# Row transfers by the sync engine at row numbers in registers, and the second tile of the last pair but one rounded as a whole ahead of the last pair's sums

## The chip, the cores and the metric

The kernel runs on one core of a Trainium2 chip. Such a core has a matrix engine (TensorE, PE in the profile, its weight loads PEld), a vector engine (VectorE, DVE), an activation engine (ScalarE, ACT), a general engine (GpSimd, POOL), a sync engine that here only issues transfers (SyncE, SP), and 16 DMA engines that move data between the device's memory and the on-chip memory. Each engine takes its instructions in order; between engines they wait for each other by semaphores. The metric is the device time of one execution in microseconds (us), given as the median of several runs.

## The reference

One gated cross-attention layer of the Flamingo kind, followed by a feed-forward layer with quantised weights and activations. There are 16 batches of 224 rows of 512 values (x), and for every batch 750 context rows of 384 values with a mask. Cut to what matters:

```python
x = x + tanh(g_xattn) * attention(layernorm(x), ctx, mask)      # 8 heads of 64, softmax over the unmasked context rows
x = x + tanh(g_ffn)   * ffn(layernorm(x))

def ffn(x):
    h = gelu(bitlinear(x, w1, b1))          # 512 -> 2048
    return bitlinear(h, w2, b2)             # 2048 -> 512

def bitlinear(x, w, b):
    xq = act_quant(rmsnorm(x))              # per row: scale 127 / max|x|, round, scale back
    wq = weight_quant(w)                    # one scale for the matrix: round to -1, 0, 1
    return xq @ wq.T + b
```

The rounding of a row needs the largest absolute value of the whole row; the mean square of the row only enters a factor that is applied behind the matrix product.

## The kernel before

**Order of the rows.** The program first sorts the 16 batches by how many context rows the mask keeps, and then works on slots (positions in that order) instead of batches. The 3584 rows of the slots, one after the other, are cut into 28 tiles of 128 rows (`NTOK`), and two tiles make a pair (`NPAIR` is 14). A slot has 224 rows, so a tile can hold the end of one slot and the beginning of the next: tiles 1, 3 and 5 of every seven do. `sh.token` is a table on the chip that holds, for each row of each tile, the number of its row in x and in the output. Rows are fetched (`fetch_x`, L807) and stored (`store`, L1488) by indirect transfers of POOL, which take the 128 row numbers of a tile out of that table. Only the last four tiles are stored otherwise: three row numbers are loaded into registers of SP (L1750 to L1759), and L1486 stores the tile from SP in one or two pieces.

**Attention.** A loop over the slots (L1711) weaves three streams of work together (`merge`, by estimated costs): the attention of slot s, the preparation of slots s+1 to s+3 (fetch and normalise x, gather the kept context rows, queries, keys and values), and the feed-forward work of an earlier pair. `scores` (L1095) makes the scores on PE, a masked copy with the row's maximum on DVE, the exponential with the row's sum on ACT, a reciprocal on DVE (L1139), and the scaling of the probabilities `p` by that reciprocal on POOL (L1140). `turn_probs` (L1155) turns `p` on PE (L1163) for the product with the values.

**Feed-forward, per pair.** `residual` fetches the rows of x again into `y` (three buffers, so a fetch must wait until the pair three before is stored) and adds a bias on POOL (L1245). `project` (L1247) multiplies by `wo` on PE (L1252) and adds onto `y` on DVE (L1255). `normalise` (L1277) makes the layer norm and the rounded `xq` on DVE and turns it by a transposing transfer of SP into `xqT` (L1302). `up` (L1324) multiplies on PE (L1333) and adds the bias on DVE (L1341). `gelu` (L1358) applies Gelu on ACT, then on DVE takes the largest absolute value (L1369), scales, rounds into 16-bit integers (L1372) and casts (L1374), giving `hq`, which a transposing transfer of SP turns into `hqT` (L1377); ACT squares the row for the mean square (L1382). `down` (L1465) multiplies on PE (L1469); the result and `y` are added on DVE (L1482), and the tile is stored.

**The tail.** Behind the loop stands the work on the last pairs, written out (L1767 to L1812). Pair 13 has functions of its own: `turn_rows` turns `xq` on PE, `up_last` works by halves of 1024 columns with the maxima by halves (L1419), `gelu_last` makes the rounding from the two maxima, and `turn_by_tensor` (L1347) turns `hq` by 16 PE transposes and two ACT copies (L1355). `mean_square` and `measure_last` make the factor of a tile on ACT and POOL. In pair 12, tile 0 is turned by SP's transfer and tile 1 by `turn_by_tensor`. Below, (12,1) is tile 1 of pair 12.

**Order.** The framework puts each engine's instructions into an order of its own, near the program's; `tc.issue_after(instruction)` makes what is inside come later in that order than the instruction, without a wait on the chip. Waits follow from the data: who reads a tile waits for who wrote it, and who overwrites it waits for its readers. Two stores of rows that are only known at run time count as writes of the same output, so that each waits until the one before has landed.

Of the kernel before, what the change touches and what calls it, by code (L numbers as in the profile page):

```python
# [11 lines left out]
ALU = mybir.AluOpType  # L12
# [722 lines left out]
def compact_path(ctx, tc, sh, x, context, out, late_loads, stages):  # L735
# [71 lines left out]
    def fetch_x(dst, t):  # L807
        nc.gpsimd.indirect_dma_start(  # L808
            out=dst,
            out_offset=None,  # L810
            in_=x_rows,
            in_offset=bass.IndirectOffsetOnAxis(ap=token(t), axis=0),
            bounds_check=B * S - 1,
            oob_is_err=False,
        )
# [177 lines left out]
    def fetch(i):  # L993
        if i:
            xp = pa.tile([P, 2, D], F32, tag="x", name=f"x_{i}", bufs=3)
        else:
            xp = early[:, : 2 * D].rearrange("p (k d) -> p k d", k=2)
        for k in range(2):
            fetch_x(xp[:, k, :], 2 * i + k)
        normed[i] = xp  # L1000
# [237 lines left out]
    def residual(i):  # L1238
# [3 lines left out]
        for k in range(2):  # L1242
            fetch_x(y[:, k, :], 2 * i + k)
# [103 lines left out]
    def turn_by_tensor(i, k):  # L1347
        f = pairs[i]
        hq, hqT = f["hq", k], f["hqT", k]
        for g in range(2):  # L1350
            pt = gen([P, NF // 2, P], BF16, f"hqp_{i}_{k}_{g}")
            for n in range(NF // 2):
                at = g * FF // 2 + n * P
                nc.tensor.transpose(pt[:, n, :], hq[:, at : at + P], ident16)
# [3 lines left out]
    def gelu(i, ks=(0, 1)):  # L1358
# [8 lines left out]
        for k in ks:  # L1367
# [8 lines left out]
            if (i, k) != (NPAIR - 2, 1):  # L1376
                nc.sync.dma_start_transpose(out=hqT, in_=hq)  # L1377
# [14 lines left out]
    def up_last(i, k):  # L1392
# [8 lines left out]
        for g in range(2):  # L1401
# [16 lines left out]
            with tc.issue_after(late["rounded"]):  # L1418
                nc.vector.tensor_reduce(most[:, g : g + 1], h[:, cols], AX.X, ALU.max, apply_absolute_value=True)  # L1419
        f["h", k], f["most", k] = h, most  # L1420
        return last.ins

# [55 lines left out]
    def store(i, k):  # L1478
# [5 lines left out]
        if i >= NPAIR - 2:  # L1484
            for p, n, at in late["pieces"][2 * i + k]:
                nc.sync.dma_start(out_rows[bass.ds(at, n), :], y[p : p + n, :])  # L1486
            return added.ins
        nc.gpsimd.indirect_dma_start(  # L1488
            out=out_rows,
            out_offset=bass.IndirectOffsetOnAxis(ap=token(2 * i + k), axis=0),  # L1490
            in_=y,
            in_offset=None,
            bounds_check=B * S - 1,
            oob_is_err=False,
        )
# [253 lines left out]

    with tc.issue_after(pairs[NPAIR - 6]["turning"].ins):  # L1750
        where = [
            nc.values_load(
                sh.token[p : p + 1, t // 7, t % 7 : t % 7 + 1],
                engines=[mybir.EngineType.SP],
                min_val=0,
                max_val=B * S - n,
            )
            for p, t, n in ((0, NTOK - 4, 64), (64, NTOK - 4, S), (32, NTOK - 2, S))
        ]  # L1759

    late["pieces"] = {
        NTOK - 4: [(0, 64, where[0]), (64, 64, where[1])],
        NTOK - 3: [(0, 128, where[1] + 64)],
        NTOK - 2: [(0, 32, where[1] + 192), (32, 96, where[2])],
        NTOK - 1: [(0, 128, where[2] + 96)],
    }
# [14 lines left out]
    with tc.issue_after(lowered):  # L1781
        for k in range(2):
            projected = project(i, k)
            normed = normalise(i, (k,))
    with tc.issue_after(normed):
        gelu(i - 1, (1,))
    measure_last(i - 1, 1)
    with tc.issue_after(projected):
        lowered = down(i - 1, 0, lambda: turn_rows(i, 0))
    with tc.issue_after(lowered):  # L1790
        up_last(i, 0)
        mean_square(i, 0)
        turn_rows(i, 1)
        raised = up_last(i, 1)
    store(i - 1, 0)
    with tc.issue_after(raised):
        turn_by_tensor(i - 1, 1)
        lowered = down(i - 1, 1)
    mean_square(i, 1)
    with tc.issue_after(gelu_last(i, 0)):  # L1800
        added = store(i - 1, 1)
    with tc.issue_after(added):
        gelu_last(i, 1)
    with tc.issue_after(raised):
        turn_by_tensor(i, 0)
    measure_last(i, 0)
    measure_last(i, 1)
    with tc.issue_after(lowered):
        down(i, 0, lambda: turn_by_tensor(i, 1))
    store(i, 0)  # L1810
    down(i, 1)
# [35 lines left out]
```

## Time and profile before

| | us |
|---|---|
| median of 3 runs | 729.25 (728.92 to 732.07) |
| profiled execution | 730.5, its span 728.4 |
| PE busy | 677.1 of the span |
| DVE, ACT, POOL busy | 495.1, 413.0, 389.3 |
| mean granted PE clock | 0.982 |
| stores by POOL (24) | 27.6 busy, 1.148 each |
| fetches of y and x by POOL (28 and 26) | 29.0 and 28.5 busy, 1.04 and 1.10 each |
| scaling of `p` by POOL (64) | 78.7 busy |

The profile is of one execution. "Busy" counts an engine's own work; a line of a group or of the timeline gives the start, the length, the engine, the line of the kernel, the operation, `output<-input` with shapes, a count, and in brackets how long the engine had stood idle before it and whose end released it. A line of the waits reads: who waited, `<-` for whom, us in total, number of times, the longest. A line of the stretches gives the busy time of each engine in that window, the clock that PE was granted (1.00 is full), the share of time that the DMA engines were busy, and GB/s. Idle time of an engine costs only where something that sets the end waits for it.

### The profile page before, as it was taken

The numbers are of one execution on the slowest core, as the hardware profiler recorded it, in microseconds if no ns is written. First come the engines' busy times: TensorE is split into PE (matmuls) and PEld (weight loads), VectorE is DVE, ScalarE is ACT, GpSimd is POOL, SyncE is SP. The second block draws the span as 40 slices with busy tenths as digits, with TensorE's granted clock in tenths as the row PEclk, the third lists the DMA queues.
The fourth block names the chain that finished last, engine by engine and source line by source line (L and its number), as shares of the span: only waits on it lengthen the run. The fifth ranks groups of instructions, "written<-read, shape, count | busy, mean of one in ns | idle before, by whom it ended". The sixth has DMA issues, their size and how long they took to land.

```text
span 728.4 us, 11444 instructions
## 1 busy us (share of the span) xinstructions
PE 677.1 (93%) x3917; PEld 432.7 (59%) x3917; DVE 495.1 (68%) x1296; ACT 413.0 (57%) x974; POOL 389.3 (53%) x545
## 2 busy tenths in 40 slices
PE   4997899999999999999799999999999999998875
PEld 3775687665666566656465566566666656554332
DVE  5495755877476475775485966747768493969883
ACT  2558554376483672774565647727466564766462
POOL 5583568454484534735646655457555445266512
PEclk9999899999999999999999999999999999999998
DMA  6884031113232222223222332113214232142301
GB/s 231 294 281 157 1 103 35 28 46 58 74 75 58 66 46 62 81 44 88 65 48 76 81 73 69 42 45 94 61 45 69 63 58 73 30 102 56 75 14 49
DMA packets 80146, 56.74 MB, mean 78 GB/s; under 512 B 68208, under 2 KB 68352, under 8 KB 79952
## 3 DMA queue, kind: packets, MB, share of 16 engines
q1 hardware_dynamic: 72336, 31.22, 18.2%
q0 software_dynamic: 7744, 24.71, 10.9%
q8 instruction: 33, 0.54, 0.3%
q14 instruction: 33, 0.27, 0.1%
HBM read 32.06 MB, written 7.34 MB: 54 GB/s over the span
## 4 chain that ended last, share of the span: by engine, by line
PE 70%; DVE 10%; issue 6%; POOL 6%; DMA 3%; ACT 3%; POOLq 0%; DVEq 0%; ACTq 0%
PE op L1252 11%; PE qp L1066 11%; PE fp L1469 11%; PE hp L1333 9%; PE kp L946 6%; PE sim L1106 5%; PE vp L962 5%; PE ptp L1163 3%; PE av L1188 3%; POOL p L1140 2%; DMA hqT<-hq 2%; POOL x L808 2%; PE xnp L1045 1%; DVE a L1369 1%; PE ctxp L935 1%
## 5 line engine op out<-in xcount | busy, mean ns | idle before, releaser
L1140 POOL TENSOR_TENSOR p<-p,rec 112x768 f32<-112x768 f32 (+2 forms) x64 | 78.7, 1230 | 76.2 <-DVE rec L1139 30.7
L1130 ACT ACTIVATE p<-p,nm 112x192 f32<-112x192 f32 (+2 forms) x256 | 104.7, 412 | 9.9 <-DVE nm L1120 6.9
L1469 PE MATMUL fp<-w2T,hqT 128*128 128x512 fp8e4 x448 | 103.3, 384 | 6.2 <-ACT hqT L1355 3.1
L1066 PE MATMUL qp<-xnT,wq_sb 128*128 128x224 f32 x512 | 105.3, 359 | 0.6 <-ACT xnT L781 0.6
L1252 PE MATMUL op<-wo_sb,xoT 128*128 128x512 f32 x224 | 103.7, 599 | 0.0
L1333 PE MATMUL hp<-w1T,xqT 128*128 128x512 fp8e4 x416 | 99.1, 382 | 2.2 <-DVE h L1341 1.0
L1066 PEld LDWEIGHTS qp<-xnT,wq_sb 128*128 128x128 f32 x512 | 97.1, 194 | 6.4 <-issue 3.1
L1341 DVE SCALAR_TENSOR_TENSOR h<-hp,c,b_bc 128x1024 f32<-128x1024 f32 x52 | 66.5, 1281 | 43.6 <-PE hp L1333 43.3
L1469 PEld LDWEIGHTS <-hqT 128*128 128x128 bf16 x448 | 42.9, 99 | 61.2 <-issue 7.0
L1120 DVE CUSTOM_DVE_ANT_0 p<-sim,mask 112x192 f32<-112x192 f32 (+2 forms) x224 | 56.1, 304 | 33.0 <-PE sim L1106 32.5
L1369 DVE TENSOR_REDUCE a<-h 128x1 f32<-128x2048 f32 x26 | 59.3, 2281 | 19.8 <-ACT h L1366 19.6
L1333 PEld LDWEIGHTS <-xqT 128*128 128x128 bf16 x416 | 39.8, 98 | 46.1 <-issue 7.0
L1482 DVE SCALAR_TENSOR_TENSOR y<-fp,c,y 128x512 f32<-128x512 f32 x28 | 20.9, 746 | 64.8 <-PE fp L1469 63.2
L1252 PEld LDWEIGHTS op<-wo_sb,xoT 128*128 128x128 f32 x224 | 40.7, 190 | 38.8 <-issue 36.4
L946 PE MATMUL kp<-ctxT,wk_sb 128*128 128x192 f32 (+1 forms) x360 | 60.4, 317 | 0.0
L1488 POOL DMA_INDIRECT out_dram<-y,token x24 | 27.6, 1148 | 57.9 <-DVE y L1482 53.6
L946 PEld LDWEIGHTS kp<-ctxT,wk_sb 128*128 128x128 f32 x360 | 54.7, 199 | 5.5 <-issue 3.8
L1382 ACT ACTIVATE h<-h 128x2048 f32<-128x2048 f32 x25 | 47.7, 1908 | 17.4 <-DVE hq L1372 12.2
L1312 POOL TENSOR_TENSOR y<-y,b_bc 128x512 f32<-128x512 f32 x28 | 36.9, 1321 | 34.5 <-DVE fx L1292 34.2
L781 ACT COPY pT<-ptp 128x448 f32<-128x448 f32 (+1 forms) x62 | 32.2, 535 | 40.3 <-PE ptp L1163 38.8
L781 ACT COPY qT<-qp 128x448 f32<-128x448 f32 x29 | 15.4, 532 | 66.4 <-PE qp L1066 66.1
L1106 PE MATMUL sim<-kT,qT 64*112 64x192 f32 (+2 forms) x512 | 50.9, 312 | 2.3 <-issue 0.9
(199 smaller groups left out, 1249.5 us busy)
## 6 DMA issues: line engine op xcount, KB each, us to landing
raw<-in_L_ffn_w_dram SPq DMA_DIRECT2D x16, 512.0 KB
wq_sb<-in_L_xattn_W_q_dram SPq DMA_DIRECT2D x1, 1024.0 KB
b_bc<-in_L_ffn_b_dram SPq DMA_DIRECT2D x1, 1024.0 KB
wk_sb<-in_L_xattn_W_k_dram SPq DMA_DIRECT2D x1, 768.0 KB
wv_sb<-in_L_xattn_W_v_dram SPq DMA_DIRECT2D x1, 768.0 KB
wo_sb<-in_L_xattn_W_o_dram SPq DMA_DIRECT2D x1, 512.0 KB
wo_sb<-in_L_xattn_W_o_dram SPq DMA_DIRECT2D x2, 256.0 KB
out_dram<-y SPq DMA_DIRECT2D x2, 256.0 KB
```

The source lines that it names most:

```text
L946: nc.tensor.matmul(pk[:, p - p0, :], lhsT=sh.wk[:, c, p * P : (p + 1) * P], rhs=st["ctxT"][:, c, :cap], start=(c == 0), stop=(c == NC - 1),)
L1066: nc.tensor.matmul(pq[:, i, :], lhsT=sh.wq[:, d, (p + i) * P : (p + i + 1) * P], rhs=st["xnT"][:, d, :], start=(d == 0), stop=(d == ND - 1),)
L1106: nc.tensor.matmul(sim[:, j, i, :cap], lhsT=st["qT"][j * DH : (j + 1) * DH, p, q * TQ : (q + 1) * TQ], rhs=keys["kT"][j * DH : (j + 1) * D ...
L1120: nc.vector.tensor_tensor_reduce(out=probs[:, h, :cap], in0=sim[:, j, i, :cap], in1=keys["mask"][:, first + j * begin : first + j * begin ...
L1130: nc.scalar.activation(probs[:, h, :cap], probs[:, h, :cap], AF.Exp, bias=nmax, scale=-1.0, accum_out=total[:TQ, h : h + 1],)
L1140: nc.gpsimd.tensor_tensor(probs[:, :, first : first + cap], probs[:, :, :cap], rec[:TQ].unsqueeze(2).to_broadcast([TQ, 4, cap]), ALU.mult,)
L1252: last = nc.tensor.matmul(po, lhsT=xoT[:, d, at : at + P], rhs=sh.wo[:, d, :], start=(d == 0), stop=(d == ND - 1))
L1333: last = nc.tensor.matmul(ph[:, n, :], lhsT=f["xqT"][:, k * ND + d, :], rhs=w1T[:, d, at : at + NB], start=(d == 0), stop=(d == ND - 1),)
L1341: nc.vector.scalar_tensor_tensor(h[:, cols], ph.rearrange("t i n -> t (i n)"), f["c1", k], sh.b1[:, cols], ALU.mult, ALU.add)
L1369: nc.vector.tensor_reduce(amax[:, k : k + 1], h, AX.X, ALU.max, apply_absolute_value=True)
L1382: nc.scalar.activation(f["h", k], f["h", k], AF.Square, accum_out=ss[:, k : k + 1])
L1469: last = nc.tensor.matmul(po, lhsT=f["hqT", k][:, n, :], rhs=w2T[:, n, :], start=(n == 0), stop=(n == NF - 1))
```

## The change

Three things change.

1. A new generator `pieces_of(t)` gives, for a tile, its one or two pieces that lie in one slot each. The first time that a slot is touched, the number of its first row is loaded from `sh.token` into a register of SP (`begins`). `fetch_x` gets a flag: with it, the rows come by direct transfers of SP at these numbers. It is set for x from tile 7 on and for every fetch of `y`. All stores go this way too. The three register loads behind the loop and the table of pieces go.
2. In the tail, `gelu(12,1)` comes before the sums and the normalising of pair 13 and not behind them. Its `hq` is now turned by SP's transfer, and that of (12,0) by PE, between the two projections of pair 13.
3. The maxima of pair 13 become a function `maxima` of their own, placed behind both `up_last`; the squares of pair 13 are placed later; `turn_rows(13,0)` and the turning of (13,1) no longer stand in the middle of another tile's `down`, but between whole ones.

```diff
--- before.py
+++ after.py
@@ -804,7 +804,31 @@
     x_rows = x.rearrange("b s d -> (b s) d")
     out_rows = out.rearrange("b s d -> (b s) d")
 
-    def fetch_x(dst, t):
+
+    begins = {}
+
+    def pieces_of(t):
+
+        p = 0
+        while p < P:
+            s, at = divmod(t * P + p, S)
+            n = min(P - p, S - at)
+            if s not in begins:
+                r = s * S
+                begins[s] = nc.values_load(
+                    sh.token[r % P : r % P + 1, r // P // 7, r // P % 7 : r // P % 7 + 1],
+                    engines=[mybir.EngineType.SP],
+                    min_val=0,
+                    max_val=B * S - S,
+                )
+            yield p, n, begins[s] + at
+            p += n
+
+    def fetch_x(dst, t, sync=False):
+        if sync:
+            for p, n, at in pieces_of(t):
+                nc.sync.dma_start(dst[p : p + n, :], x_rows[bass.ds(at, n), :])
+            return
         nc.gpsimd.indirect_dma_start(
             out=dst,
             out_offset=None,
@@ -996,7 +1020,7 @@
         else:
             xp = early[:, : 2 * D].rearrange("p (k d) -> p k d", k=2)
         for k in range(2):
-            fetch_x(xp[:, k, :], 2 * i + k)
+            fetch_x(xp[:, k, :], 2 * i + k, 2 * i + k >= 7)
         normed[i] = xp
 
     def norm(i, ks=(0, 1)):
@@ -1240,7 +1264,7 @@
         f = pairs[i] = {}
         f["y"] = y = late["rows"].tile([P, 2, D], F32, tag="y", name=f"y_{i}", bufs=3)
         for k in range(2):
-            fetch_x(y[:, k, :], 2 * i + k)
+            fetch_x(y[:, k, :], 2 * i + k, True)
         for k in range(2):
             nc.gpsimd.tensor_tensor(y[:, k, :], y[:, k, :], sh.bo, ALU.add)
 
@@ -1351,7 +1375,7 @@
             pt = gen([P, NF // 2, P], BF16, f"hqp_{i}_{k}_{g}")
             for n in range(NF // 2):
                 at = g * FF // 2 + n * P
-                nc.tensor.transpose(pt[:, n, :], hq[:, at : at + P], ident16)
+                f["turned"] = nc.tensor.transpose(pt[:, n, :], hq[:, at : at + P], ident16).ins
             turned = nc.scalar.copy(hqT[:, g * NF // 2 : (g + 1) * NF // 2, :], pt)
         return turned.ins
 
@@ -1373,7 +1397,7 @@
             f["hqT", k] = hqT = late["rows"].tile([P, NF, P], BF16, tag="hqT", name=f"hqT_{i}_{k}", bufs=2)
             late["rounded"] = nc.vector.tensor_copy(hq, hq.bitcast(I16)).ins
             f["hq", k] = hq
-            if (i, k) != (NPAIR - 2, 1):
+            if (i, k) != (NPAIR - 2, 0):
                 nc.sync.dma_start_transpose(out=hqT, in_=hq)
         if (i, ks[0]) == (NPAIR - 2, 1):
             f["a2", 1] = amax[:, 1:2]
@@ -1415,10 +1439,16 @@
                 h[:, cols], ph.rearrange("t i n -> t (i n)"), f["c1", k], sh.b1[:, cols], ALU.mult, ALU.add
             )
             nc.scalar.activation(h[:, cols], h[:, cols], AF.Gelu)
-            with tc.issue_after(late["rounded"]):
-                nc.vector.tensor_reduce(most[:, g : g + 1], h[:, cols], AX.X, ALU.max, apply_absolute_value=True)
         f["h", k], f["most", k] = h, most
         return last.ins
+
+    def maxima(i, k):
+        f = pairs[i]
+        for g in range(2):
+            cols = slice(2 * g * NB, 2 * (g + 1) * NB)
+            nc.vector.tensor_reduce(
+                f["most", k][:, g : g + 1], f["h", k][:, cols], AX.X, ALU.max, apply_absolute_value=True
+            )
 
     def gelu_last(i, k):
 
@@ -1481,18 +1511,9 @@
         y = f["y"][:, k, :]
         added = nc.vector.scalar_tensor_tensor(y, po, f["c2", k], y, ALU.mult, ALU.add)
         load["v"] += 700
-        if i >= NPAIR - 2:
-            for p, n, at in late["pieces"][2 * i + k]:
-                nc.sync.dma_start(out_rows[bass.ds(at, n), :], y[p : p + n, :])
-            return added.ins
-        nc.gpsimd.indirect_dma_start(
-            out=out_rows,
-            out_offset=bass.IndirectOffsetOnAxis(ap=token(2 * i + k), axis=0),
-            in_=y,
-            in_offset=None,
-            bounds_check=B * S - 1,
-            oob_is_err=False,
-        )
+        for p, n, at in pieces_of(2 * i + k):
+            nc.sync.dma_start(out_rows[bass.ds(at, n), :], y[p : p + n, :])
+        return added.ins
 
     NPAIR = NTOK // 2
 
@@ -1746,24 +1767,6 @@
             scores(s + 1, 0)
             scores(s + 1, 1)
 
-
-    with tc.issue_after(pairs[NPAIR - 6]["turning"].ins):
-        where = [
-            nc.values_load(
-                sh.token[p : p + 1, t // 7, t % 7 : t % 7 + 1],
-                engines=[mybir.EngineType.SP],
-                min_val=0,
-                max_val=B * S - n,
-            )
-            for p, t, n in ((0, NTOK - 4, 64), (64, NTOK - 4, S), (32, NTOK - 2, S))
-        ]
-
-    late["pieces"] = {
-        NTOK - 4: [(0, 64, where[0]), (64, 64, where[1])],
-        NTOK - 3: [(0, 128, where[1] + 64)],
-        NTOK - 2: [(0, 32, where[1] + 192), (32, 96, where[2])],
-        NTOK - 1: [(0, 128, where[2] + 96)],
-    }
     i = NPAIR - 1
     residual(i)
     with tc.issue_after(late["av"]), tc.issue_after(late["rounded"]):
@@ -1778,37 +1781,46 @@
     with tc.issue_after(raised):
         lowered = down(i - 2, 1)
     store(i - 2, 1)
-    with tc.issue_after(lowered):
-        for k in range(2):
-            projected = project(i, k)
-            normed = normalise(i, (k,))
+    gelu(i - 1, (1,))
+    with tc.issue_after(late["rounded"]):
+        with tc.issue_after(lowered):
+            projected = project(i, 0)
+        normed = normalise(i, (0,))
+        with tc.issue_after(projected):
+            turn_by_tensor(i - 1, 0)
     with tc.issue_after(normed):
-        gelu(i - 1, (1,))
+        with tc.issue_after(pairs[i - 1]["turned"]):
+            projected = project(i, 1)
+        normalise(i, (1,))
     measure_last(i - 1, 1)
     with tc.issue_after(projected):
-        lowered = down(i - 1, 0, lambda: turn_rows(i, 0))
+        lowered = down(i - 1, 0)
     with tc.issue_after(lowered):
-        up_last(i, 0)
-        mean_square(i, 0)
+        turn_rows(i, 0)
+        raised = up_last(i, 0)
+    with tc.issue_after(raised):
         turn_rows(i, 1)
         raised = up_last(i, 1)
+    maxima(i, 0)
     store(i - 1, 0)
     with tc.issue_after(raised):
-        turn_by_tensor(i - 1, 1)
         lowered = down(i - 1, 1)
-    mean_square(i, 1)
+    mean_square(i, 0)
     with tc.issue_after(gelu_last(i, 0)):
+        maxima(i, 1)
         added = store(i - 1, 1)
     with tc.issue_after(added):
         gelu_last(i, 1)
-    with tc.issue_after(raised):
+    with tc.issue_after(lowered):
         turn_by_tensor(i, 0)
+        lowered = down(i, 0)
+    mean_square(i, 1)
     measure_last(i, 0)
     measure_last(i, 1)
     with tc.issue_after(lowered):
-        down(i, 0, lambda: turn_by_tensor(i, 1))
+        turn_by_tensor(i, 1)
+        down(i, 1)
     store(i, 0)
-    down(i, 1)
     store(i, 1)
 
 
```

## The prediction

> **What bounds the kernel now.** I read first the busy times, then PE's idle time by releaser, then the stretches around its long gaps, then the tail on PE and SP.
>
> ```profile
> PE 677.1 (93%) x3917; PEld 432.7 (59%) x3917; DVE 495.1 (68%) x1296; ACT 413.0 (57%) x974; POOL 389.3 (53%) x545
> ...
> PE ptp L1163 <- POOL p L1140: 15.8, 11, 4.2
> ```
>
> PE holds 677 of 728.4 us, so a gain must come out of PE's 51 idle us or its slow clock. The largest releaser of idle PE is POOL's scaling of the probabilities (L1140): 15.8 us in 11 waits. By the timeline of PE these are 4.23 us before 60.98, 1.11 before 205.37, 1.40 before 254.96, 1.46 before 302.89, 3.55 and 0.47 before 349.77 and 353.77, 0.97 before 398.13, 0.35, 0.43 and 1.02 between 434 and 453, and 0.78 before 662.58.
>
> The stretches around two of the gaps (length, PE, PEld, DVE, ACT, POOL busy, granted clock, DMA):
>
> ```profile
> 57.00:61.00 4.00, 0.01 (x1) 0.02 (x1) 3.43 (x5) 3.98 (x8) 3.67 (x4) 1.00 0.98 337
> 61.00:66.00 5.00, 5.00 (x34) 3.43 (x35) 1.00 (x3) 2.89 (x5) 1.35 (x1) 0.66 0.37 147
> ...
> 346.00:350.00 4.00, 0.45 (x4) 0.26 (x4) 0.00 (x0) 3.29 (x3) 3.82 (x4) 1.00 0.17 49
> 350.00:355.00 5.00, 4.53 (x20) 2.16 (x18) 1.67 (x2) 1.01 (x3) 4.45 (x6) 0.66 0.39 108
> ```
>
> A gap costs more than itself: the granted clock is 0.66 in the 5 us behind it. What POOL did ahead of the 3.55 us gap:
>
> ```profile
> 337.85 1.09 POOL L1488 DMA_INDIRECT out_dram<-y,token  x1 [4.41 <-DVE y L1482]
> 340.96 1.08 POOL L808 DMA_INDIRECT y<-in_x_dram,token  x1 [2.02 <-DMA out_dram<-y,token]
> 342.35 1.01 POOL L808 DMA_INDIRECT y<-in_x_dram,token  x1 [0.31 <-issue]
> 344.57 1.29 POOL L1245 TENSOR_TENSOR y<-y,bo_bc 128x512 f32<-128x512 f32 x1 [1.21 <-DMA y<-in_x_dram,token]
> ...
> 348.25 1.47 POOL L1140 TENSOR_TENSOR p<-p,rec 112x768 f32<-112x768 f32 x1
> 349.88 1.04 POOL L808 DMA_INDIRECT x<-in_x_dram,token  x1 [0.16 <-issue]
> 351.22 0.99 POOL L808 DMA_INDIRECT x<-in_x_dram,token  x1 [0.30 <-issue]
> 352.24 1.48 POOL L1140 TENSOR_TENSOR p<-p,rec 112x768 f32<-112x768 f32 x1
> ```
>
> The reciprocals that the two L1140 need ended at 343.65 and 345.86 on DVE. POOL came 4.6 and 6.4 us late: it issued row transfers, stood for a store to land, and stood for rows to arrive.
>
> The tail, on PE, DVE and SP:
>
> ```profile
> 689.76 1.90 PE L1469 MATMUL fp<-w2T,hqT 128*128 128x512 fp8e4 x8 [2.26 <-DMA hqT<-hq]
> 702.55 1.07 PE L1354 MATMUL hqp<-ident,hq 128*128 128x128 bf16 x16 [0.83 <-DVE hq L1374]
> 706.02 5.31 PE L1469 MATMUL fp<-w2T,hqT 128*128 128x512 fp8e4 x16 [2.39 <-ACT hqT L1355]
> 717.73 0.75 DVE L1482 SCALAR_TENSOR_TENSOR y<-fp,c,y 128x512 f32<-128x512 f32 x1 [2.85 <-PE fp L1469]
> ...
> 718.51 0.35 SPq L1486 DMA_DIRECT2D out_dram<-y  x1
> 720.63 0.32 SPq L1486 DMA_DIRECT2D out_dram<-y  x1
> 724.62 0.35 SPq L1486 DMA_DIRECT2D out_dram<-y  x1
> ```
>
> PE waits for a transfer that turns hq(12,0), then for hq(12,1), rounded late, then for ACT; the 16 matmuls at 706.02 take 5.31 us where others take 3.63. The end hangs on SP: tile 26 leaves in two pieces 2.12 us apart, and tile 27 only when the second has landed, 3.99 later, although its sum ended at 721.93. So the end is the sum of tile 26 (718.48) plus 9.9 us. Pairs are numbered 0 to 13; (12,0) is the first tile of pair 12.
>
> **The change, part by part.**
>
> Rows off POOL. All 28 y fetches, 24 stores and the 21 x fetches from tile 7 on leave POOL, at 1.04, 1.12 and 1.01 us each, 77 us of POOL. Most lies where nobody waits; what counts is what stands ahead of a late L1140.
> - Gap at 57: two x fetches (tiles 8, 9) hold POOL from 53.95 to 58.18, while the reciprocals were there at 54.22 and 56.81. Without them the second context fetch (0.95) ends about 54.9 and the first L1140 (1.46) about 56.4, ahead of PE's 56.75. Worth 4.23, plus 1.2 for matmuls at the low clock (8 of L1188 took 1.76 where the others take 0.98, 4 of L1163 took 1.01 instead of 0.60). DVE is 9.4 tenths busy there with weights, so I take 4.5 of 5.4.
> - Gaps at 205, 255, 303: the second L1140 stands behind two x fetches (2.4 us with their pauses), its reciprocal 4.7 us old. The gaps are 1.11, 1.40 and 1.46, and ten of L946 behind the first take 3.41 where 1.75 is usual, with more at low clock after them: 2.3. Against it, in these three slots the store that frees y is cut in two (tiles 1, 3, 5 cross a batch), so y comes later (below). I take 2.0, 0.9 and 0.9 of 3.4, 1.4 and 1.46.
> - Gap at 347: the store that frees y (tile 7) is whole. Issued at 337.6, landed 2.1 later (the spacing of the two pieces above), y rows in two pieces landed 2.6 after that, L1245 twice and the context fetch (3.6) end near 346.0, L1140 near 347.4 instead of 349.7; the second near 348.9, before PE's 353.3. 3.55 and 0.47 go down to about 1.2, and with them 1.4 of low clock (8 of L1333 took 2.89 instead of 1.89, L1163 0.96). I take 4.2.
> - 0.97 at 398 and 0.35 at 434: the same kind, 1.3. The two at 450 and 453 follow their reciprocals (448.60, 450.89) at once: nothing. The 0.78 at 662 stands behind POOL arithmetic: nothing.
> Sum: 4.5 + 2.0 + 0.9 + 0.9 + 4.2 + 1.3 = 13.8; the ends are 6 (the x fetches ahead of the gaps from 205 on save nothing, the rest half) and 20 (every gap above with its low clock).
>
> Rows onto SP. Some 110 direct transfers, 6 of them there already, at 0.36 plus two small register steps (0.08), and 16 loads of a row number at 0.44 plus 0.17, about 60 us of SP over the span. SP is idle most of the time: the longest of its waits for an hq cast is 28.7 us. Three waits are new on SP. A cut store's second piece waits for the first to land (2.1 to 2.4); a y fetch waits for its old store (2.0, now POOL's 22.3 us of "POOL y L808 <- DMA out_dram<-y,token"); a fetch of x waits for nothing now. Behind them on SP stand the transposing transfers, and behind those PE. The order in time is kind: at 382.15 the xqT transfer goes out, at 386.2 the second store would, at 388.4 the y fetch, and the next hqT is at 403.5. The closest is a first store at 377.2, just behind the hqT issue at 376.54 and five ahead of xqT, whose matmuls start 7 us later. Two transfers have no slack: PE waits 0.56 at 381.74 and 0.40 at 645.32. Bounds: 0 to 12 us (one us in each of 12 slots); I take 2, nearest to these two waits.
>
> The Trainium skill, "DMA: Bandwidth & Descriptors", section "Issuing engines are not separate DMA queues", speaks against this half: another issuing engine saves only the issue time, which it calls usually small beside the transfer. By it only the 1.0 us issues leave the path, the waits for landings stay, and the gap at 347 would give the shorter issues alone, 2.0 instead of 4.2, the sum 11.6 instead of 13.8. The trace has POOL standing 22.3 us for landings in front of unrelated work, and that wait moves to an engine with nothing urgent behind it, so I keep the trace's sum.
>
> The tail. gelu(12,1) with reduce 2.28, scale 0.37, round 1.29 and cast 0.69 goes ahead of normalise(13,0). DVE is then: cast of (12,0) ends 682.8 as now, that of (12,1) at 687.3 (702.5 now), xq of (13,0) about 691.3 (688.8 now), xq of (13,1) about 695.3 (694.7 now).
> - hq(12,0) is turned by PE (16 transposes, 0.9) between the two projections, and copied by ACT behind the squares at 686 to 688. Its down starts at 688.4 instead of 689.76, runs unbroken to 691.9, and the 2.26 wait goes.
> - up(13,0): turn and copy (0.4 + 0.6) from 692.0, matmuls 693.0 to 696.6; up(13,1): 697.6 to 701.2.
> - hq(12,1) goes by SP's transfer at 687.4; at 6.74 us, as the one at 682.98 took, it lands by 694.2, so down(12,1) runs 701.2 to 704.8. Now it ends at 711.33.
> - DVE then sets the pace: four bias adds at 1.28, two maxima at 1.2, the sum of (12,0) at 0.75, all from 695.3 without a hole, then scale and rounding (2.65): hq(13,0) by 706. Turn, ACT copies (1.0 each), down(13,0) 707 to 711; its factor comes over ACT's squares and six POOL steps, some 5 us from the last square in the trace, at about 712. So the sum of tile 26 ends near 712.4, not 718.48.
> - Turning hq(13,1) is no longer hidden inside down(13,0): 0.5 + 1.0 + 3.6 + 0.75 behind hq(13,1) (711.7) gives 717.5. SP's chain asks for tile 27 only at 712.4 + 2.1 + 4.0 = 718.5, so this is covered by 1 us; without the cover it would cost its excess.
> - The moved maxima and squares are the same instructions, counted above; the removed early loads of row numbers (three of 0.44) lay on an idle SP.
> Gain 6.1. Bounds: -2 (DVE order worse, clock low for 3 us) to 9 (every PE gap after 687 and the slow 1.7).
>
> **Sum.** The profiled execution is 730.5 us (span 728.4 and 2.1 around it), 1.25 above the median of 729.25. 13.8 - 2 + 6.1 = 17.9: 712.6 on its own time, 711.3 on the median's. I say 712.
>
> **The rivals.**
> 1. Only the tail pays. L1140 comes earlier, but PE then stands for ACT's exponentials or DVE, or y arrives later through cut stores and L1245 still stands ahead of L1140. For it: the waits at 450 and 453 followed the reciprocal directly. Against it: elsewhere the reciprocals are 2.8 to 6.4 us old. 730 - 6 - 2 = 722.
> 2. Slower: SP's in-order waits hold the transposing transfers. If the order on SP puts a store or a y fetch ahead of an hqT, that hqT waits 2.1 to 4.5 us, PE with it, in up to 12 slots and twice in a slot. It decides from where the mean delay past the slack exceeds 17.9 + 2 over 12, 1.7 us per slot; at 2.2 us per slot, 730 + 26 - 20 = 736. Against it are the distances named above. [...]
> 3. No change: the two halves give back what they gain (y late at every slot, 14; tail bound by DVE, 6): 729.
>
> **How the numbers follow.** Both halves pay 0.67 (702 to 720); only the tail 0.16 (720 to 725.6); no change 0.06; slower 0.11. A difference under 0.5% (3.6 us) can't be told from none. Faster 0.83, same 0.06, slower 0.11. The low end is 730.5 - 20 - 9 = 702; the high end takes in rival 1 and the slow side of no change, to 728, and leaves out rival 2 and some 0.05 below.
>
> **What would show it.** Right: PE's wait for L1140 falls from 15.8 us to under 5; no POOL transfer for y or output is left; the stretch 57 to 61 is busy at full clock; down(12,1) follows up(13,1) without a gap; the last three stores keep their spacing but begin some 18 us earlier. Wrong: PE idle ended by hqT or xqT in most slots; SP waits for out_dram in front of transposes; L1245 waiting longer for y; a PE gap before the turn of hq(13,0) of over 3 us.

## The result, and the profile after

The changed kernel takes 786.54 us (median; 782.59 to 790.69) against 728.47 us (727.04 to 732.07) for the kernel before: a ratio of 1.0786, with a 95% interval of 1.0759 to 1.0813. It is 58 us slower; the forecast was 712, with a range of 702 to 728. The profiled execution has a span of 784.6 us against 728.4, and a mean granted clock of 0.953 against 0.982. In the changed kernel L1140 has become L1164, L1163 is L1187 (PE's turn of the scaled probabilities), L1245 is L1269, L1255 is L1279, L1312 is L1336, L808 is L830 and L1486 is L1515.

The busy times of the page, and from the waits of all engines (total us, number of waits, longest) four rows that grew and lead to the cause:

```profile
PE 690.8 (88%) x3917; PEld 441.7 (56%) x3917; DVE 490.7 (63%) x1296; ACT 414.5 (53%) x974; POOL 310.5 (40%) x472
...
POOL p L1164 <- DVE rec L1163: 138.3, 26, 17.7
...
PE ptp L1187 <- POOL p L1164: 57.4, 12, 13.1
...
DVE y L1279 <- POOL y L1269: 32.0, 4, 9.0
POOL y L1269 <- DMA y<-in_x_dram: 21.8, 9, 5.9
```

POOL did lose its 79 us of row transfers, 389.3 down to 310.5, and yet PE's wait for POOL's scaling rose from 15.8 to 57.4 us. The 56.2 us of longer span are 42.5 of idle PE (51.3 before, 93.8 now) and 13.7 of longer busy PE, for the same 3917 matmuls at a lower clock; the wait for the scaling alone, up by 41.6, is nearly all of the idle part. The first row of the waits tells that POOL is not the culprit this time: it stands for a reciprocal of DVE (138.3 us, 30.7 before). The last two rows lead on: DVE stands for POOL's y, and POOL for the y rows to arrive.

PE's timeline has the large waits, four of them with a smaller one behind three (start, length, what runs, idle time before it and its releaser):

```profile
160.10 1.01 PE L1187 MATMUL ptp<-ident,p 112*128 112x112 f32 x4 [10.33 <-POOL p L1164]
163.55 1.01 PE L1187 MATMUL ptp<-ident,p 112*128 112x112 f32 x4 [2.06 <-POOL p L1164]
...
227.86 1.01 PE L1187 MATMUL ptp<-ident,p 112*128 112x112 f32 x4 [11.12 <-POOL p L1164]
231.57 1.01 PE L1187 MATMUL ptp<-ident,p 112*128 112x112 f32 x4 [2.32 <-POOL p L1164]
...
294.80 1.01 PE L1187 MATMUL ptp<-ident,p 112*128 112x112 f32 x4 [12.95 <-POOL p L1164]
298.10 1.01 PE L1187 MATMUL ptp<-ident,p 112*128 112x112 f32 x4 [1.92 <-POOL p L1164]
...
552.00 1.01 PE L1187 MATMUL ptp<-ident,p 112*128 112x112 f32 x4 [13.12 <-POOL p L1164]
```

These seven are 53.8 of the 57.4 us. All other waits for the scaling together are 3.6 us, where before they were 15.8: what the prediction wanted to remove was removed, and something larger came in at four places. Two stretches of the prediction, and those around the first large gap (length, PE, PEld, DVE, ACT, POOL busy, granted clock, DMA share, GB/s):

```profile
57.00:61.00 4.00, 3.03 (x28) 2.23 (x26) 4.00 (x5) 4.00 (x13) 2.32 (x2) 1.00 0.93 321
61.00:66.00 5.00, 4.09 (x28) 2.51 (x27) 5.00 (x17) 5.00 (x11) 1.47 (x1) 1.00 0.78 251
...
150.00:160.00 10.00, 0.00 (x0) 0.00 (x0) 5.54 (x11) 4.38 (x18) 5.17 (x4) 0.75 0.27 84
160.00:165.00 5.00, 2.84 (x13) 2.49 (x14) 4.53 (x10) 1.19 (x3) 4.28 (x7) 0.50 0.00 0
165.00:170.00 5.00, 5.00 (x17) 4.18 (x17) 0.00 (x0) 1.53 (x5) 2.91 (x6) 0.64 0.23 52
```

57 to 61, empty on PE before, now has PE busy for 3.03 of 4 us, at full clock. From 150 to 160 PE does nothing at all.

Now the second large gap, followed back through POOL and SP. First SP's waits in the whole run, then its row transfers ahead of the gap with the turn on PE that it waits for, then POOL and DVE:

```profile
SPq L830 <- PE xnp L1069: 115.9, 10, 59.7
...
SPq L1515 <- DMA out_dram<-y: 29.5, 18, 2.9
```

```profile
207.72 2.51 SPq L1515 DMA_DIRECT2D out_dram<-y  x2
...
211.13 0.66 PE L1069 MATMUL xnp<-ident,x 128*128 128x128 f32 x4 [0.57 <-ACT ctxT L781]
...
211.91 1.42 SPq L830 DMA_DIRECT2D x<-in_x_dram  x3
213.53 1.74 SPq L830 DMA_DIRECT2D y<-in_x_dram  x3
...
218.72 2.49 POOL L1269 TENSOR_TENSOR y<-y,bo_bc 128x512 f32<-128x512 f32 x2 [3.90 <-DMA y<-in_x_dram]
...
220.02 0.75 DVE L1279 SCALAR_TENSOR_TENSOR y<-op,tgates,y 128x512 f32<-128x512 f32 x1 [8.42 <-POOL y L1269]
...
224.94 0.17 DVE L1163 RECIPROCAL rec<-sum 112x4 f32<-112x4 f32 x1
...
226.33 1.48 POOL L1164 TENSOR_TENSOR p<-p,rec 112x768 f32<-112x768 f32 x1
```

Read from the end: PE resumes at 227.86 when POOL has scaled p. POOL could not before DVE's reciprocal at 224.94 and a bias add of its own that stood ahead (1.27 us). DVE had stood 8.42 us at the sum of projection and y (L1279), which stands ahead of the reciprocal in its order. The sum waited for POOL's y + b_o, that for the y rows, and these were asked for at 213.53, directly behind the x fetch. The x fetch waits for an x buffer: there are three, and the last reader of the one it will overwrite is PE's turn xnp, which ends at 211.79 here, 0.12 us before the fetch. So SP stands ten times for PE, 115.9 us in all and 59.7 at the longest (in front of 146.62), and what is behind x on SP stands with it: y. Before the change POOL asked for pair 0's y at 102.34; now SP asks for it at 148.37.

### The profile page after: what moved, and what is told of

Same layout as the page of the kernel before. It is cut to its first block, busy times and chain, and to the rows that moved or that the text cites. A ratio compares the mean times of both kernels' runs of the same rounds, so it can differ in the third digit from the quotient of the medians.

```text
span 784.6 us, 11697 instructions
## 1 busy us (share of the span) xinstructions
PE 690.8 (88%) x3917; PEld 441.7 (56%) x3917; DVE 490.7 (63%) x1296; ACT 414.5 (53%) x974; POOL 310.5 (40%) x472
## 4 chain that ended last, share of the span: by engine, by line
PE 69%; DVE 14%; DMA 5%; ACT 5%; POOL 4%; issue 2%; SPq 1%; DVEq 0%; POOLq 0%; ACTq 0%
PE qp L1090 10%; PE hp L1357 10%; PE fp L1499 10%; PE op L1276 10%; PE kp L970 6%; PE vp L986 5%; PE sim L1130 5%; PE av L1212 3%; DMA y<-in_x_dram 2%; PE ptp L1187 2%; DVE a L1393 2%; DMA hqT<-hq 2%; PE xnp L1069 2%; PE vr L997 1%; PE ctxp L959 1%
## 5 line engine op out<-in xcount | busy, mean ns | idle before, releaser
L1164 POOL TENSOR_TENSOR p<-p,rec 112x768 f32<-112x768 f32 (+2 forms) x64 | 79.6, 1245 | 191.1 <-DVE rec L1163 138.3
L1090 PE MATMUL qp<-xnT,wq_sb 128*128 128x224 f32 x512 | 108.6, 367 | 0.6 <-ACT xnT L781 0.6
L1499 PE MATMUL fp<-w2T,hqT 128*128 128x512 fp8e4 x448 | 101.4, 379 | 3.1 <-ACT hqT L1379 1.3
L1090 PEld LDWEIGHTS qp<-xnT,wq_sb 128*128 128x128 f32 x512 | 99.7, 199 | 7.0 <-issue 2.9
L1187 PE MATMUL ptp<-ident,p 112*128 112x112 f32 (+1 forms) x256 | 37.9, 277 | 57.9 <-POOL p L1164 57.4
L1499 PEld LDWEIGHTS <-hqT 128*128 128x128 bf16 x448 | 42.5, 98 | 57.5 <-issue 6.4
L1187 PEld LDWEIGHTS ptp<-ident,p 112*128 112x128 f32 (+1 forms) x256 | 30.2, 147 | 71.1 <-POOL p L1164 61.2
L970 PE MATMUL kp<-ctxT,wk_sb 128*128 128x192 f32 (+1 forms) x360 | 64.6, 331 | 0.0
L1406 ACT ACTIVATE h<-h 128x2048 f32<-128x2048 f32 x25 | 47.7, 1910 | 30.3 <-DVE hq L1396 19.5
L932 POOL DMA_INDIRECT ctx<-in_ctx_dram,keys x21 | 23.9, 1139 | 100.6 <-PE ctxp L959 65.0
L970 PEld LDWEIGHTS kp<-ctxT,wk_sb 128*128 128x128 f32 x360 | 59.0, 211 | 5.0 <-issue 3.8
L1390 ACT ACTIVATE h<-h 128x2048 f32<-128x2048 f32 x25 | 47.7, 1910 | 25.8 <-DVE h L1365 25.6
```

Of the source, the lines that this page charges most:

```text
L970: nc.tensor.matmul(pk[:, p - p0, :], lhsT=sh.wk[:, c, p * P : (p + 1) * P], rhs=st["ctxT"][:, c, :cap], start=(c == 0), stop=(c == NC - 1),)
L1090: nc.tensor.matmul(pq[:, i, :], lhsT=sh.wq[:, d, (p + i) * P : (p + i + 1) * P], rhs=st["xnT"][:, d, :], start=(d == 0), stop=(d == ND - 1),)
L1164: nc.gpsimd.tensor_tensor(probs[:, :, first : first + cap], probs[:, :, :cap], rec[:TQ].unsqueeze(2).to_broadcast([TQ, 4, cap]), ALU.mult,)
L1187: nc.tensor.transpose(pt[: at.stop, h, :], probs[:, h, c : c + at.stop], ident[:TQ, :TQ])
L1390: nc.scalar.activation(f["h", k], f["h", k], AF.Gelu)
L1499: last = nc.tensor.matmul(po, lhsT=f["hqT", k][:, n, :], rhs=w2T[:, n, :], start=(n == 0), stop=(n == NF - 1))
```

## The experiments

The theory: **an x fetch that waits for PE's turn holds the y fetch behind it on SP**, and late y stops DVE, POOL and PE in that order. Against it stood the prediction's second rival in a wider form (what SP's waits hold are the transposing transfers, or the cut stores that wait piece for piece, 29.5 us). All ratios are to the kernel before, run beside the experiment.

**Ask for y ahead of the slot.** Only the place in the program is other; every transfer stays on SP.

```diff
             if complete:
-                flow.append((0.0, lambda i=projected: residual(i)))
+                residual(projected)
```

> The changed kernel with one line moved: the y fetch of a pair stands in the program ahead of the slot's x fetch, not behind it. Theory A: on SP an x fetch waits for PE to turn the tile that is in its buffer, up to 59.7 us, the y fetch stands behind it, and POOL and DVE stand for y in front of the softmax's reciprocal and scaling; that makes the four PE gaps of 12 to 15 us (53.8 us of idle, and the slow clock behind each). Then y comes early, the four gaps go, and the time is 708 to 720. Rival B: y is late because stores cut in two wait for each other on SP (29.5 us in 18 waits) and fetches wait for stores. These stay, so the time stays at 775 to 790.

Measured: 708.61 us (707.04 to 709.05), ratio 0.9697 (0.9662 to 0.9733). Its waits for the scaling, and SP's row fetches around the place of the first gap:

```profile
PE ptp L1187 <- POOL p L1164: 2.2, 3, 1.0
```

```profile
99.68 1.43 SPq L830 DMA_DIRECT2D y<-in_x_dram  x3
140.04 1.37 SPq L1326 DMA_TRANSPOSE xqT<-xq  x1
148.18 1.40 SPq L830 DMA_DIRECT2D x<-in_x_dram  x3
149.77 1.70 SPq L830 DMA_DIRECT2D y<-in_x_dram  x3
```

y of pair 0 goes out at 99.68, and the y behind the x fetch at 149.77 is already that of the next pair, which the changed kernel asks for at 213.53. The stores are cut as in the changed kernel and the transposes share the queue, so the 78 us between the two versions belong to the order of x and y alone.

**Take away what x waits for: a fourth x buffer.** The order stays that of the changed kernel.

```diff
-            xp = pa.tile([P, 2, D], F32, tag="x", name=f"x_{i}", bufs=3)
+            xp = pa.tile([P, 2, D], F32, tag="x", name=f"x_{i}", bufs=4)
...
-            junk = pa.tile([P, 2, D], F32, tag="x", name=f"sq_{name}_{g}", bufs=3)
+            junk = pa.tile([P, 2, D], F32, tag="x", name=f"sq_{name}_{g}", bufs=4)
```

> The changed kernel with four buffers for x instead of three, nothing else. Theory A: an x fetch then waits for a tile that was turned a pair earlier, so it waits little or not at all, though it still stands ahead of y: the four gaps go and the time is 708 to 722. Theory A', the place of the x fetch alone (its issue and its bytes in front of y) makes y late, not its wait: 780 to 790. Rival B: 775 to 790.

Measured: 708.27 us (707.77 to 712.45), ratio 0.9717 (0.9672 to 0.9761); the longest of SP's waits for PE is 15.1 us instead of 59.7, and PE waits 5.2 us for the scaling. The same gain by another way, without touching the order.

**Leave x on POOL**, with y and stores on SP:

```diff
-            fetch_x(xp[:, k, :], 2 * i + k, 2 * i + k >= 7)
+            fetch_x(xp[:, k, :], 2 * i + k)
```

> The changed kernel with all x fetches back on POOL; y fetches and stores stay on SP. Theory A (an x fetch that waits holds SP): no x fetch is left on SP, the four gaps go, and the time is 712 to 722, some us more than with y ahead, since POOL issues x again in front of the scaling (4.2 us of PE idle at 57). Rival B (cut stores and fetches that wait for stores): 775 to 790 as now.

Measured: 718.33 us (717.25 to 719.58), ratio 0.984 (0.9803 to 0.9876). The large gaps are gone here too. Two of over 2 us are left. One, 2.92 us before 62.48, stands behind the x issues, which are on POOL again. The other has another reason, POOL's wait for the y rows:

```profile
339.00 1.27 POOL L1269 TENSOR_TENSOR y<-y,bo_bc 128x512 f32<-128x512 f32 x1 [10.62 <-DMA y<-in_x_dram]
...
344.39 0.77 PE L1187 MATMUL ptp<-ident,p 112*128 112x112 f32 x4 [2.16 <-POOL p L1164]
```

**Leave y on POOL**, with x and stores on SP:

```diff
-            fetch_x(y[:, k, :], 2 * i + k, True)
+            fetch_x(y[:, k, :], 2 * i + k)
```

> Here y is fetched by POOL as before, while x fetches and stores are issued by SP. Theory (a fetch of x that waits for PE holds only the y behind it): x still waits on SP for PE, over 100 us in sum and near 60 the longest, and PE has no gap of 10 us; 712 to 724, as POOL gets its 1.0 us y issues back and waits for landed stores. Prediction's rival (what is held on SP and stops PE are transposing transfers or stores): the same long wait still stops PE, and the time stays above 735.

Measured: 712.56 us (711.34 to 713.19), ratio 0.9779 (0.9745 to 0.9812). Here SP still waits for PE in front of x, with transposing transfers and stores behind it and no y:

```profile
PE ptp L1187 <- POOL p L1164: 7.7, 7, 3.0
```

```profile
SPq L830 <- PE xnp L1069: 67.7, 10, 17.1
```

The expectation of such waits, over 100 us in sum and near 60 the longest, was a miss: with y in time a transposing transfer stands ahead of x (137.99, then x at 146.14), and part of the long wait is put down to that. So the rival is answered for waits of up to 17.1 us: transposes and stores behind an x that waits so long do not stop PE. A wait of 59.7 us without a y behind it did not occur in any run.

**Only pair 0's y ahead of its slot.** This asks whether one late y is handed on, or each slot loses its own time.

```diff
-                flow.append((0.0, lambda i=projected: residual(i)))
+                if projected == 0:
+                    residual(0)
+                else:
+                    flow.append((0.0, lambda i=projected: residual(i)))
```

> The changed kernel with only pair 0's y asked for ahead of its slot. If each slot loses its own time, because in each its y stands behind its own x: the first gap of 10.3 + 2.1 us goes with its low clock, the other three stay; 768 to 776. If the lateness starts with pair 0 and is handed on by the buffers of y and POOL's order: the gaps from 227 to 298 go with it, at most the one near 552 stays; 708 to 730.

Measured: 769.17 us (766.36 to 771.45), ratio 1.0563 (1.0523 to 1.0602). PE's timeline keeps three of the four:

```profile
205.81 1.01 PE L1187 MATMUL ptp<-ident,p 112*128 112x112 f32 x4 [13.01 <-POOL p L1164]
...
272.73 1.01 PE L1187 MATMUL ptp<-ident,p 112*128 112x112 f32 x4 [13.50 <-POOL p L1164]
...
530.74 1.01 PE L1187 MATMUL ptp<-ident,p 112*128 112x112 f32 x4 [12.52 <-POOL p L1164]
```

Each slot loses its own time: its y stands behind its own x. The gap near 160 is gone with SP's longest wait (16.1 us now). The ones at 205.81, 272.73 and 530.74 are those at 227.86, 294.80 and 552.00 of the changed kernel, 21 to 22 us earlier.

**Both remedies**, the diffs of the first two experiments together:

> Both remedies at once: y asked for ahead of the slot and a fourth x buffer. Theory: they take away the same wait, so together they give what one does, 705 to 710, within 3 us of either. If each takes away a different cost, the gains add beyond that: under 704.

Measured: 710.48 us (709.54 to 711.26), ratio 0.9749 (0.9714 to 0.9784). That is 0.5 us above the expected range and no more gain than either alone: they take away the same wait.

**Rows and tail apart.** First the tail alone: the changed kernel with the x, y and mid-stream transfers, and the early row numbers of the tail's stores, as in the kernel before.

```diff
-            fetch_x(xp[:, k, :], 2 * i + k, 2 * i + k >= 7)
+            fetch_x(xp[:, k, :], 2 * i + k)
...
-            fetch_x(y[:, k, :], 2 * i + k, True)
+            fetch_x(y[:, k, :], 2 * i + k)
...
-        for p, n, at in pieces_of(2 * i + k):
-            nc.sync.dma_start(out_rows[bass.ds(at, n), :], y[p : p + n, :])
-        return added.ins
+        if i >= NPAIR - 2:
+            for p, n, at in late["pieces"][2 * i + k]:
+                nc.sync.dma_start(out_rows[bass.ds(at, n), :], y[p : p + n, :])
+            return added.ins
+        nc.gpsimd.indirect_dma_start(
+            out=out_rows,
+            out_offset=bass.IndirectOffsetOnAxis(ap=token(2 * i + k), axis=0),
...
```

> The kernel before with the tail of the changed one (second tile of pair 12 rounded ahead, maxima, squares and turns moved); rows move as before, by POOL. The two traces give 59.6 us before and 54.5 after from the start of up(12,0) to the end. If the tail pays on its own: 722 to 725, ratio about 0.993. Rival C, the tail costs and the shorter end comes from stores and clock: 727 or more.

Measured: 726.48 us (724.22 to 731.25), ratio 0.9943 (0.9922 to 0.9964). The median lies between the two expectations; as a ratio the gain is clear of noise, but small (0.4 to 0.8%). Then y first with all row moves, and the tail of the kernel before (its lines behind the last slot, its exception in the rounding and its maxima inside `gelu`):

```diff
-    gelu(i - 1, (1,))
-    with tc.issue_after(late["rounded"]):
-        with tc.issue_after(lowered):
-            projected = project(i, 0)
-        normed = normalise(i, (0,))
...
+    with tc.issue_after(lowered):
+        for k in range(2):
+            projected = project(i, k)
+            normed = normalise(i, (k,))
+    with tc.issue_after(normed):
+        gelu(i - 1, (1,))
...
```

> All of the change's row moves with y asked for ahead of the slot, and the tail of the kernel before. It splits the 21.7 us that y-first gained on the kernel before (730.3 to 708.6) into rows and tail. If the halves add, as the prediction's sum took them, this is 708.6 plus the tail's gain, measured alone as 3.8 and between the traces as 5.1: 712 to 714, and the rows are worth 16 to 18 us with y in time against the 11.8 (13.8 - 2) of the prediction. If the new tail gains only because rows have left POOL, or loses by it, it is under 710 or over 717.

Measured: 709.97 us (708.33 to 711.53), ratio 0.974 (0.9702 to 0.9778). That is below the 712 to 714 of halves that add: the rows are worth 2.6% by themselves, and what the tail adds to them (0.974 to 0.9697) is within the intervals, which overlap. In the profiles the part from up(12,0) to the end is 59.6 us before, 58.1 here, 57.2 with the tail alone and 54.7 with both, so in these single profiles rows and tail help each other at the end (1.5 and 2.4 us alone, 4.9 together); the times do not resolve that.

**Which of the row moves pays.** With y first, the stores of pairs 0 to 11 back on POOL, so that the fetches alone are on SP:

```diff
+        if i < NPAIR - 2:
+            nc.gpsimd.indirect_dma_start(
+                out=out_rows,
+                out_offset=bass.IndirectOffsetOnAxis(ap=token(2 * i + k), axis=0),
+                in_=y,
...
+            )
+            return added.ins
         for p, n, at in pieces_of(2 * i + k):
```

> y asked for ahead of the slot, x and y fetches on SP, but the stores of pairs 0 to 11 back on POOL, whole and at about 1.1 us each. If the fetches alone carry the gain (POOL stands for nothing that lands, as the wait for a landed store is SP's now): 708 to 712. If each issue on POOL in front of the scaling of probabilities counts: one of 1.1 us in most slots and its low clock behind, 714 to 720, with PE waits for that scaling over 6 us.

Measured: 709.6 us (708.14 to 712.05), ratio 0.9702 (0.9654 to 0.9751). And x alone on SP, with y fetches and these stores on POOL, in the changed kernel's order:

```diff
-            fetch_x(y[:, k, :], 2 * i + k, True)
+            fetch_x(y[:, k, :], 2 * i + k)
...
+        if i < NPAIR - 2:
+            nc.gpsimd.indirect_dma_start(
+                out=out_rows,
...
         for p, n, at in pieces_of(2 * i + k):
```

> Only the x fetches from tile 7 on are issued by SP, with the changed tail; y fetches and stores of pairs 0 to 11 stay on POOL as before the change. Theory: an x fetch that stands for PE holds nothing that PE needs, so there is no gap of 10 us. If the parts add, moving x is worth the 9.7 us by which x on POOL was worse than y-first (718.3 against 708.6), and the tail 3.8: 714 to 719, with the gap near 57 gone and the one near 347 left. If the x fetches were worth only the gap near 57 (4.5 in the prediction): 720 to 724.

Measured: 724.18 us (722.16 to 726.29), ratio 0.9908 (0.9877 to 0.994). The waits of PE, SP and POOL in these two, first with the stores on POOL:

```profile
PE ptp L1187 <- POOL p L1164: 2.2, 3, 1.0
...
SPq L830 <- PE xnp L1069: 110.0, 10, 17.2
SPq L830 <- DMA out_dram<-y,token: 29.2, 4, 7.9
```

and with x alone on SP:

```profile
PE ptp L1187 <- POOL p L1164: 12.9, 10, 3.6
...
SPq L830 <- PE xnp L1069: 116.0, 10, 19.1
POOL y L832 <- DMA out_dram<-y,token: 23.1, 11, 2.6
```

With x alone on SP, PE's timeline has no gap near 57 any more, but the others are left, of which these are the largest:

```profile
201.87 0.60 PE L1187 MATMUL ptp<-ident,p 112*128 112x112 f32 x4 [2.13 <-POOL p L1164]
252.86 0.60 PE L1187 MATMUL ptp<-ident,p 112*128 112x112 f32 x4 [1.26 <-POOL p L1164]
...
301.31 0.60 PE L1187 MATMUL ptp<-ident,p 112*128 112x112 f32 x4 [1.38 <-POOL p L1164]
348.19 0.60 PE L1187 MATMUL ptp<-ident,p 112*128 112x112 f32 x4 [3.56 <-POOL p L1164]
```

Two things follow. SP's wait for PE is 116.0 us here and 110.0 with the stores on POOL, as much as the 115.9 of the slow kernel, and neither has a large gap: the price of a wait on an in-order queue is what stands behind it, not its length. And the gaps from 201 to 302 come from the y fetch on POOL, which stands for a landing store (23.1 us): they stay when x leaves POOL, and they go when y leaves, with x on SP or on POOL. The one at 348 is gone with y first, but with x on POOL 2.16 us of it were left. The expectation that the parts add was wrong for x: the time fell just above the other range, 720 to 724.

## Why the prediction was wrong, and where it was right

**The step that failed** is in "Rows onto SP": "a fetch of x waits for nothing now". It waits for PE's last turn of the tile still in its buffer, ten times, for 115.9 us. In the sum SP's waits stood at 2 us; with y behind that wait they cost 78 (786.54 against 708.61 us with y first). The step listed three waits and priced the two that the trace of before shows as waits. This one was there too, but unseen: POOL was busy or stood in its own order until after the turn, so its x fetch found the buffer free and the gap ahead of it was listed as "issue". The trace of before shows one such pair, the turn that frees the buffer and the fetch:

```profile
196.82 0.60 PE L1045 MATMUL xnp<-ident,x 128*128 128x128 f32 x4
...
201.46 1.03 POOL L808 DMA_INDIRECT x<-in_x_dram,token  x1 [0.15 <-issue]
```

Counted through that trace, the freeing turn ends 0.3 to 7.1 us ahead of the first x fetch of each of the ten pairs from pair 4 on (4.0 us here); on SP the fetch stood until the turn had ended. The question "what frees the destination?", put to the code (three buffers, last read by L1069), would have found it. So a wait that a busy engine hides can be laid bare when the operation moves to an idle one.

**"Behind them on SP stand the transposing transfers, and behind those PE"** named the wrong neighbour. The y fetch stands directly behind x. The rest of the sentence's worry cost little: in the changed kernel PE waits 1.3 us for hqT transfers.

**The rivals.** The second had the right kind, SP's in-order waits, and the right sign, with the wrong object. It priced the held transfer at 2.2 us in each of 12 slots, and gave 736; four slots with 12 to 15 us of idle PE each, and the low clock behind them, gave 786. It had 0.11. No term of the sum stood for a wait on SP that lasts until the next turn on PE, here up to 59.7 us, so the range could not hold the result.

**"Rows off POOL", 13.8.** With y in time this half is right in sign and too small. Up to the start of up(12,0) the y-first kernel is 16.5 us ahead of the kernel before (652.33 against 668.78), against 13.8 - 2 = 11.8 in the prediction. Without the new tail the same row moves gave a ratio of 0.974, some 19 us. Of the 16.5 us, 12.2 are less idle PE and 4.2 are shorter busy PE (632.8 to 628.5 us for the same 3702 matmuls). The prediction's own rows add up to 13.5 us of gaps and 4.9 of low clock, and it took 13.8 of these 18.4; what it took off for DVE, for cut stores and for late y was too much. The -2 for SP is not to be seen.

- Gap at 57 (4.5): right in its mechanism. It is gone with x alone on SP, and 2.92 us are left with x on POOL; the time with x alone, 0.9908 beside 0.9943 for the tail alone, agrees but does not resolve it. Other POOL work can open the gap again: with a fourth x buffer, and no x fetch on POOL there, 3.00 us stand before 59.77, behind two context fetches of 2.42 and 1.67 us.
- Gaps at 205, 255, 303 (2.0, 0.9, 0.9): removed, but not by the step named. They were put down to x fetches in front of L1140; with x alone on SP, 2.13, 1.26 and 1.38 are left. They belong to the y fetch on POOL and its wait for the landing store.
- Gap at 347 (4.2): the landing wait in front of unrelated work was read rightly, and it stays at 3.56 with x alone on SP. That it goes with y on SP is true in part. It is gone with y first, stores on POOL or not; but 2.16 us are left with x on POOL and 2.36 with both remedies, where POOL's add of the bias (L1269) stands ahead of the scaling and waits 10.6 and 11.1 us for the y rows.

**The page's rule.** The Trainium skill ("DMA: Bandwidth & Descriptors", "Issuing engines are not separate DMA queues") says that another issuing engine saves only the sequencer's issue time. For the issues of the stores the runs agree: the stores on POOL or on SP make no measurable difference (709.6, ratio 0.9702, and 708.61, ratio 0.9697). For the waits in front of the issues they don't: with the y fetches and their landing wait off POOL the gaps of 1.3 to 3.6 us went, and putting x's wait in front of y on SP cost 78 us.

**The tail, 6.1.** From up(12,0) to the end it gives 5.1 in the two profiles (59.6 to 54.5 us), and 3.8 in the medians of the tail alone. On PE, POOL and DVE, the changed kernel:

```profile
759.93 3.63 PE L1430 MATMUL hp<-w1T,xqT 128*128 128x512 fp8e4 x16 [0.68 <-ACT xqT L1346]
763.39 3.62 PE L1499 MATMUL fp<-w2T,hqT 128*128 128x512 fp8e4 x16
...
772.57 0.40 POOL L1485 TENSOR_TENSOR r<-sq 128x1 f32<-128x1 f32 x1 [8.31 <-ACT sq L1478]
...
774.79 0.75 DVE L1512 SCALAR_TENSOR_TENSOR y<-fp,c,y 128x512 f32<-128x512 f32 x1 [1.20 <-POOL c L1298]
778.77 0.75 DVE L1512 SCALAR_TENSOR_TENSOR y<-fp,c,y 128x512 f32<-128x512 f32 x1 [3.23 <-PE fp L1499]
```

down(12,1) follows up(13,1) without a gap, and its 16 matmuls take 3.62 us instead of 5.31, as said. The sum of tile 26 was to end near 712.4, which is 773.7 here (up(12,0) starts 61.3 later); it ends at 775.5, and 1.20 us of the difference is its wait for POOL's factor. The term for that factor was too small: put at about 712, which is 773.3 here, it was ready at 774.75. The squares that POOL stood for, 8.31 us, are those of tile 27: in POOL's order their sum stands ahead of the factor of tile 26, whose own inputs were there at 765.6. This is the same pattern as on SP, a wait in front of work that does not need it; no run tests what the other order would give. From that sum to the end it takes 9.1 us instead of 9.9.

## What to carry to other kernels

Before a transfer is moved to another engine's queue, list for it and for all that will stand behind it when its source is ready and when its destination is free, from the code and not from the waits that the profile shows: a busy engine can hide the waits of its own transfers. On a queue that works in order put the transfers in the order in which their waits end; a prefetch that waits for a buffer belongs behind what is needed in this slot, or needs one buffer more. Here one line of order was worth 78 us, and with it the changed kernel is 3% faster than the kernel before instead of 8% slower.

## What the hardware showed that was not expected

The clock's price is not only in the long gaps. Behind the gap of 10.33 us the clock is 0.50 from 160 to 165 and 0.64 from 165 to 170, and the second gap, of 2.06 us at 163.55, falls into this low stretch. All in all the changed kernel's PE is busy 13.7 us longer for the same 3917 matmuls, with 53.8 us of such gaps. The Trainium skill ("TensorE: Matmul & The Clock Gate", "Part 1: The HAM clock gate") says that full clock comes back after about 3.4 us of sustained work. In the kernel before, by stretches of 1 us, the clock is 0.50 from 61 and back at full near 64.4, 3.4 us after PE resumed at 60.98, which agrees; in the changed kernel it is 0.50 up to 168 and back at full near 168.6, some 5 us after PE resumed at 163.55, so there it took longer. One stretch of the kernel before, then two of the changed one (the third number from the end is the clock):

```profile
64.00:65.00 1.00, 1.00 (x12) 0.86 (x12) 0.12 (x1) 0.47 (x2) 0.00 (x0) 0.79 0.00 0
...
167.00:168.00 1.00, 1.00 (x5) 1.00 (x5) 0.00 (x0) 0.00 (x0) 1.00 (x2) 0.50 0.00 1
168.00:169.00 1.00, 1.00 (x4) 0.80 (x3) 0.00 (x0) 0.20 (x1) 0.03 (x1) 0.70 0.00 0
```

Every x fetch's wait for PE on SP is part of a good kernel too: 110 us of it in one of 709.6 us. The sum of a wait row on a queue says nothing of its cost until the rows behind it are known.
